# Recurrence of a selective scan: products and turn in one TensorE step with 64x64 diagonals

## The chip, the cores and the metric

The kernel runs on one core of one Trainium2 chip. The metric is the device time of one execution in microseconds (us). Engines are named as the profile names them: PE (TensorE matmul), PEld (TensorE weight load), DVE (VectorE), ACT (ScalarE), POOL (GpSimd), SP (SyncE, which here issues DMAs).

## The reference, cut to what matters

Four layers run one after another on an image of 2 x 128 x 128 pixels with 128 channels: window attention, a Fourier layer with a feed-forward, a complex-valued recurrence, and a four-direction selective scan. The change lies in the fourth. Its scan, for each of four directions k and each of 256 channels d with 16 states n, is

```
delta = softplus(delta + delta_bias)
def step(h, inp):                      # over time
    ut, dt, bt, ct = inp
    dA = jnp.exp(dt[..., None] * A4)
    h = dA * h + (dt * ut)[..., None] * bt[:, :, None, :]
    y = jnp.einsum('bkdn,bkn->bkd', h, ct)
    return (h, y)
```

So per time step and direction there are 256 x 16 states; `dA` is a factor for each of them, and the term added is the product of `delta u` (by channel) and `B` (by state). Two of the four directions go through the pixels by columns, and two of them backwards. The image is scanned in 32 x 32 windows.

## The kernel before, in words

`layer3_conv` (L1120 to L1242) makes the convolved input u, window by window, and stores it in DRAM twice with channels on partitions (`xs`, one copy by rows and one by columns) and once with pixels on partitions (`xst`, 1024 pixels x 256 channels a window).

`layer3_scan` (L1245 on) goes through 256 parts: 2 images x 4 directions x 16 windows x 2 halves of 512 time steps (T = 512). A part has eight slots, and a slot is four scans of 128 x 512: 128 partitions hold 4 states x 32 channels, so 32 such tiles make up a part's 256 x 16 states. The whole stage is written out in order by hand: `in_order` chains each engine's instructions in the order of the program text, so nothing is moved by a scheduler. Slot g issues, in this order:

- `exponentials(g + 1)` (L1518): four ACT activations of 128 x 512, dA from the spread delta `db` and a scale by partition.
- `kept(g - 1)` (L1594): ACT copies the last column of the four scanned tiles into the state kept for the next part.
- `products(g + 2)` (L1537, L1542): delta u (`du`, time on partitions) times B (`bt`, by partition), for a quarter of the states and half of the time, eight instructions of 128 x 256; of the 64 of a part ACT does 50 and POOL 14. The result `but` has time on partitions.
- `weighted(g - 1)` (L1600): POOL multiplies the four scanned tiles by C (`cb`), 128 x 2048 in one instruction.
- `tiles(g)`: four times, four PE transposes (L1574) turn 128 x 128 blocks of `but` into a PSUM tile `ups` of 128 x 512 (three buffers of one bank), and DVE scans it (L1582, `tensor_tensor_scan`: state = da * state + ups).
- `sums(g - 2)` (L1556): four PE matmuls with the selector `sel` (128 x 32) add up the states into `yps`, one for each 32 channels, on four column tiles.

A table `steps` places the rest of a part's work at slots relative to the part's first, at the head or end of a slot or after its scan number 0 to 3: `load_x` and `load_u` (SP loads), `project` (L1346) and `projected` (L1355, a DVE copy of 40 x 512 out of PSUM, and a store of C to DRAM), `turn_b` (L1364) and `turned_b` (L1371), `ranks` (L1378), `softplus` (L1389, ACT, with a change of the activation table before and after), `spread` (SP: delta to DRAM and back into `db` and `cb`, spread over partitions), `turn` (L1416) and `turned` (L1426: du = u times delta, DVE), `skip` (L1448, L1453, DVE), and for the backward directions `unturn` (L1477) and `store` (L1487, two DVE copies of 128 x 512, then a store of the pixels). PSUM's eight banks go to `ups` (3), `yps` (2) and a pool `ps_m` for the rest (3).

Of the kernel before, what the change touches and what calls it, by code (L numbers as in the profile page):

```python
# [16 lines left out]
NB = 2  # L17
# [1102 lines left out]
def layer3_conv(tc, cs, ins, x3, xs, xst, sc, sh):  # L1120
# [11 lines left out]
    with ExitStack() as ctx:  # L1132
# [20 lines left out]
        for b in range(NB):  # L1153
            for hg in range(4):
# [62 lines left out]
                for wg in range(4):  # L1217
# [24 lines left out]
                    nc.sync.dma_start(xst[b, hg, wg].rearrange("(t p) d -> p t d", p=P), xt)  # L1242


def layer3_scan(tc, cs, ins, xs, xst, yc, ys):  # L1245
# [13 lines left out]
    with ExitStack() as ctx:  # L1259
# [6 lines left out]
        five = pool("l3b_five", 5)  # L1266
        ps_u = pool("l3b_ps_u", 3, space=PSUM)
        ps_y = pool("l3b_ps_y", 1, space=PSUM)
        ps_m = pool("l3b_ps_m", 3, space=PSUM)
# [15 lines left out]

        dsk = w.tile([P, 2, 2, 2], F32, name="dsk")
# [28 lines left out]

        def load_x(i):
            b, k, s, sub = parts[i]
            _, (hg, wg) = place(i)
            xc = four.tile([P, 2, T], F32, name=f"xc_{tag_of(i)}", tag="xc")
            nc.sync.dma_start(xc, xs[k % 2, b, hg, wg, :, :, sub * T : sub * T + T])  # L1320
            held[i] = {"xc": xc}

        def load_u(i):
            b, k, s, sub = parts[i]
            _, (hg, wg) = place(i)
            ut = one.tile([P, 4, 256], F32, name=f"ut_{tag_of(i)}", tag="ut")
            px = xst[b, hg, wg]
            if k % 2:
                cols = px.rearrange("(h t w) d -> w h t d", h=32, w=4)
                for w4 in range(4):  # L1330
                    nc.sync.dma_start(
                        ut[32 * w4 : 32 * w4 + 32], cols[w4, :, 4 * sub : 4 * sub + 4, :]
                    )
            else:
                nc.sync.dma_start(
                    ut, px.rearrange("(t p) d -> p t d", p=P)[:, 4 * sub : 4 * sub + 4, :]
                )
            held[i]["ut"] = ut
# [13 lines left out]
        def projected(i):  # L1352
            v = held[i]
            xd = xds[i % 2]
            nc.vector.tensor_copy(xd[0:NX, :], v["xps"][0:NX, :])  # L1355
            v["cd"] = dr.tile([NS, T], F32, name=f"cd_{tag_of(i)}", tag="cd")
            nc.sync.dma_start(v["cd"], xd[DR + NS : NX, :])
            v["xd"] = xd

        def turn_b(i):  # L1360
            v = held[i]
            v["bps"] = ps_m.tile([P, 4, NX], F32, name=f"btps_{tag_of(i)}", tag="misc")
            for j in range(4):
                nc.tensor.transpose(  # L1364
                    v["bps"][:, j, :], v["xd"][0:NX, j * P : (j + 1) * P], cs.ident[0:NX, 0:NX]
                )
# [42 lines left out]
        def turn(g):  # L1409
            def f(i):  # L1410
                v = held[i]
                tps = ps_m.tile([P, 2, 2, P], F32, name=f"dltps_{tag_of(i)}_{g}", tag="misc")
                for j in range(2):
                    for e in range(2):
                        p0 = (2 * g + j) * P
                        nc.tensor.transpose(tps[:, j, e, :], v["dl"][:, e, p0 : p0 + P], cs.ident)  # L1416
                v.setdefault("tps", []).append(tps)
            return f
# [62 lines left out]
        def store(i):  # L1481
# [4 lines left out]
            for g in range(2):  # L1486
                nc.vector.tensor_copy(  # L1487
# [7 lines left out]
            (-12, "end", load_x), (-10, "end", load_u),  # L1495
            (-8, 1, project(0)), (-8, 2, project(1)), (-7, 0, projected),
            (-6, 0, turn_b), (-6, 1, ranks(0)), (-6, 2, ranks(1)),
            (-5, "head", softplus), (-5, 0, turned_b), (-5, 1, spread),
            (-4, 0, turn(0)), (-4, 1, turn(1)), (-3, 0, turned(0)), (-3, 1, turned(1)),
            (6, "end", load_forth), (9, 3, skip(0)), (10, 3, skip(1)),  # L1500
# [9 lines left out]

        def exponentials(g):
            i, s = divmod(g, 8)
            q, e = divmod(s, 2)
            k = parts[i][1]
            da = three.tile([P, 4, T], F32, name=f"da_{tag_of(i)}_{s}", tag="da")
            for j in range(4):
                c = 8 * q + 4 * e + j
                nc.scalar.activation(  # L1518
                    da[:, j, :], held[i]["db"][:, 4 * e + j, :], AF.Exp, scale=na[:, k, c : c + 1]
# [3 lines left out]
        def products(g):  # L1523

            i, s = divmod(g, 8)
            q, half = divmod(s, 2)
            v = held[i]
            but = five.tile([P, 2, 8, 4, 32], F32, name=f"but_{tag_of(i)}_{s}", tag="but")
            v[("but", q, half)] = but
            bt = v["bt"]  # L1530
            du = v["du"].rearrange("p t (g c) -> p t g c", c=32)
            for j in range(2):
                tb = 2 * half + j
                for n in range(4):
                    c = DR + 4 * q + n
                    if n == 3 and (tb < 3 or q % 2):
                        nc.gpsimd.tensor_tensor(  # L1537
                            but[:, j, :, n, :], du[:, tb],
                            bt[:, tb, c : c + 1].unsqueeze(2).to_broadcast([P, 8, 32]), ALU.mult,
                        )  # L1540
                    else:
                        nc.scalar.activation(  # L1542
                            but[:, j, :, n, :], du[:, tb], AF.Copy, scale=bt[:, tb, c : c + 1]
                        )

        def sums(g):
            i, s = divmod(g, 8)
            q, e = divmod(s, 2)
            v = held[i]
            if q == 0:  # L1550
# [3 lines left out]
            hs = v.pop(("hs", s))  # L1554
            for j in range(4):
                nc.tensor.matmul(  # L1556
                    v["yps"][e][32 * j : 32 * j + 32, :], sel, hs[:, j, :],
                    start=(q == 0), stop=(q == 3),
                )

        def tiles(g):
            i, s = divmod(g, 8)
            q, e = divmod(s, 2)
# [5 lines left out]
            hs = three.tile([P, 4, T], F32, name=f"hs_{tag_of(i)}_{s}", tag="hs")  # L1569
            c0 = 8 * q + 4 * e  # L1570
            for j in range(4):
                ups = ps_u.tile([P, T], F32, name=f"ups_{tag_of(i)}_{s}_{j}", tag="ups")
                for tb in range(4):
                    nc.tensor.transpose(  # L1574
                        ups[:, tb * P : (tb + 1) * P],
                        v[("but", q, tb // 2)][:, tb % 2, 4 * e + j].rearrange("p n c -> p (n c)"),
                        cs.ident,
                    )
                o, a, u = hs[:, j, :], da[:, j, :], ups
                if rev:  # L1580
                    o, a, u = o[:, ::-1], a[:, ::-1], u[:, ::-1]
                nc.vector.tensor_tensor_scan(  # L1582
                    o, a, u, state[:, c0 + j : c0 + j + 1], ALU.mult, ALU.add
                )
                at(g, j)
            v[("hs", s)] = hs

        def kept(g):

            i, s = divmod(g, 8)  # L1590
# [5 lines left out]
        def weighted(g):  # L1596
            i, s = divmod(g, 8)
            v = held[i]
            hs = v[("hs", s)]
            nc.gpsimd.tensor_tensor(  # L1600
                hs, hs, v["cb"][:, s // 2, :].unsqueeze(1).to_broadcast([P, 4, T]), ALU.mult
# [3 lines left out]
        with in_order(tc):  # L1605
            for g in range(-15, slots + 7):
# [5 lines left out]
                at(g, "mid")  # L1612
                if 0 <= g + 2 < slots:
                    products(g + 2)
# [7 lines left out]
                if 0 <= g - 2 < slots:  # L1622
                    sums(g - 2)
# [118 lines left out]
def program(tc, ins, out):  # L1742
    nc = tc.nc
    with ExitStack() as ctx:
# [7 lines left out]
        xst = dram.tile([NB, 4, 4, 1024, 256], F32, name="xst")  # L1752
# [102 lines left out]
```

## Time and profile before

| | us |
|---|---|
| median of 3 runs | 18088.65 (18087.1 to 18094.28) |
| profiled execution, its own time | 18087.3 |
| its span, first to last instruction | 18085.5 |
| first and last start of a scan (L1582) | 6150.6 and 17564.9 |

The mean granted TensorE clock of the profiled execution is 0.921. Over the whole span PE is busy 79%, DVE 84%, ACT 82% and POOL 65%; the scan stage is the last two thirds, and there the shares are higher. In a line of the profile's groups stand source line, engine, operation, output and inputs, shapes and count, then busy time and mean duration (ns) of one, then idle time before it and what ended it. In a line of the order of time stand start, duration of a run of like instructions, engine, line, and their number (x4); start-to-start times can be read off from it. A PE matmul on fp32 data that isn't a transpose appears as two records, and so does its weight load.

### The profile page before, as it was taken

To read this page: it belongs to the slowest core of one execution; us is meant where nothing else is said; L and a number is where in the kernel's file an instruction comes from. 1 tells how busy PE (TensorE), PEld (TensorE's weight loads), DVE (VectorE), ACT (ScalarE), POOL (GpSimd) and SP (SyncE) were. 2 spreads that over 40 slices of the span, in tenths; PEclk is the share of its full clock that TensorE was granted. 3 is DMA by queue.
4 is the path that set the end of the run, shared out by engine and by line. 5 is a ranking of instruction groups with operands and counts; after the bars stand their busy time and mean duration, and the time that the engine had idled before them with its cause. 6 is when DMAs were issued, how large, how long until landed. Compare 5 with 4: busy or idle time off the path is not lost. (4 is left out here: it accounts for less than half of the span.)

```text
span 18085.5 us, 277215 instructions
## 1 busy us (share of the span) xinstructions
PE 14352.7 (79%) x97794; PEld 8372.0 (46%) x97794; DVE 15201.1 (84%) x19449; ACT 14804.6 (82%) x29537; POOL 11720.3 (65%) x6490
## 2 busy tenths in 40 slices
PE   7888888888667777788877778877778887778878
PEld 5555555674223344444444444444444444444445
DVE  5766666345998899999999999999999999999986
ACT  4665666324555799999999999999999999999984
POOL 0000000011000399999999999999999999999981
PEclk9999999889889899999999999999999989999989
DMA  2000000121114544455544455554455555455556
GB/s 45 24 22 24 17 17 17 56 74 54 53 55 153 178 118 119 123 131 132 132 118 118 119 131 131 131 125 118 118 126 130 132 128 122 118 121 129 129 136 192
DMA packets 1232635, 1859.30 MB, mean 103 GB/s; under 512 B 124877, under 2 KB 591565, under 8 KB 1228942
## 3 DMA queue, kind: packets, MB, share of 16 engines
q1 hardware_dynamic: 1157374, 1817.40, 38.8%
q10 hardware_dynamic: 73872, 24.16, 0.5%
q8 instruction: 776, 12.71, 0.3%
q14 instruction: 613, 5.02, 0.1%
HBM read 1396.64 MB, written 444.60 MB: 102 GB/s over the span
## 5 line engine op out<-in xcount | busy, mean ns | idle before, releaser
L1582 DVE TENSOR_TENSOR_SCAN hs<-da,states,ups 128x512 f32<-128x512 f32 x8192 | 9845.1, 1258 | 761.8 <-PE ups L1574 746.7
L1600 POOL TENSOR_TENSOR hs<-hs,cb 128x2048 f32<-128x2048 f32 x2048 | 9327.2, 4554 | 153.9 <-ACT states L1594 151.4
L1574 PE MATMUL ups<-ident,but 128*128 128x128 f32 x32768 | 5572.7, 301 | 1913.2 <-DVE hs L1582 1334.7
L1574 PEld LDWEIGHTS ups<-ident,but 128*128 128x128 f32 x32768 | 3905.8, 151 | 5401.7 <-DVE hs L1582 3557.5
L1542 ACT ACTIVATE but<-du,bt 128x256 f32<-128x256 f32 x12800 | 5328.9, 496 | 2.4 <-DVE du L1426 1.8
L1518 ACT ACTIVATE da<-db,na 128x512 f32<-128x512 f32 x8192 | 5220.9, 709 | 3.1
L1556 PE MATMUL yps<-hs,sel 128*32 128x512 f32 x16384 | 2370.6, 653 | 509.8 <-POOL hs L1600 506.4
L1537 POOL TENSOR_TENSOR but<-du,bt 128x256 f32<-128x256 f32 x3584 | 2145.5, 619 | 10.2 <-DVE du L1426 10.2
L306 POOL TENSOR_TENSOR xres<-xres,rowb 128x256 f32<-128x256 f32 x128 | 94.3, 737 | 2466.9 <-DMA xres<-in_x 1956.5
L391 ACT COPY pT<-tps 128x512 f32<-128x512 f32 x1280 | 722.1, 584 | 1111.7 <-PE tps L386 1111.6
L386 PE MATMUL tps<-ident,s 128*128 128x128 f32 x8192 | 1229.6, 288 | 434.0 <-DVE pT L389 269.2
L358 DVE CUSTOM_DVE_ANT_1 s<-sps,relbias 128x512 f32<-128x512 f32 x2048 | 1320.5, 682 | 138.5 <-PE sps L341 133.0
L386 PEld LDWEIGHTS tps<-ident,s 128*128 128x128 f32 x8192 | 901.3, 144 | 1028.2 <-issue 499.0
L371 ACT ACTIVATE s<-s,nm 128x1024 f32<-128x1024 f32 x1024 | 1163.7, 1138 | 129.3 <-DVE nm L369 126.5
L1556 PEld LDWEIGHTS yps<-hs,sel 128*32 128x32 f32 x16384 | 332.7, 111 | 939.1 <-POOL hs L1600 711.9
L1156 POOL MEMSET xpad<- 128x34 f32 x8 | 1.3, 163 | 1169.0 <-PE xs L1030 1104.6
L341 PE MATMUL sps<-kc,qT 32*128 32x512 f32 x4096 | 619.3, 673 | 1.9 <-DVE qT L326 1.2
L389 DVE COPY pT<-tps 128x512 f32<-128x512 f32 x768 | 527.4, 687 | 59.2 <-PE tps L386 57.1
L1346 PE MATMUL xdps<-xc,xpw 128*40 128x512 f32 x1024 | 541.1, 610 | 13.2 <-DMA xpw<-in_x_projT 13.2
L734 POOL TENSOR_TENSOR xr<-xr,row_ln_b 128x512 f32<-128x512 f32 x64 | 81.2, 1270 | 708.6 <-DMA xr<-x 475.8
L1378 PE MATMUL dtps<-xd,dtw 65*128 65x512 f32 x1024 | 526.6, 595 | 0.0
L404 PE MATMUL ops<-pT,v 128*32 128x128 f32 x16384 | 500.3, 274 | 0.0
(283 smaller groups left out, 15132.6 us busy)
## 6 DMA issues: line engine op xcount, KB each, us to landing
db<-dd SPq DMA_DIRECT2D x1024, 512.0 KB
cb<-cd SPq DMA_DIRECT2D x1024, 256.0 KB
xc<-xs SPq DMA_DIRECT2D x256, 512.0 KB
dd<-dl SPq DMA_DIRECT2D x256, 512.0 KB
ut<-xst SPq DMA_DIRECT2D x128, 512.0 KB
yc<-ysb SPq DMA_DIRECT2D x128, 512.0 KB
yf<-yc SPq DMA_DIRECT2D x128, 512.0 KB
ys<-yt SPq DMA_DIRECT2D x128, 512.0 KB
```

What stands on the lines that cost most here:

```text
L341: nc.tensor.matmul(sps, v["qT"][hp, qt * P : (qt + 1) * P], kc[b, wh + g][hp, ww : ww + 2].rearrange("p a r c -> p (a r c)"), start=True, ...
L358: nc.vector.tensor_tensor_reduce(blocks(v["s", qt][:, h, 512 * g : 512 * g + 512]), blocks(v["sps", qt, g][h]), bias[:, h, :, r0 : r0 + WS ...
L371: nc.scalar.activation(s[:, h, :], s[:, h, :], AF.Exp, bias=nm[:, 2, h : h + 1], scale=-1.0, accum_out=v["sums"][:, qt, h : h + 1],)
L386: nc.tensor.transpose(tps[:, j, :], v["s", qt][:, h, k0 : k0 + P], cs.ident)
L391: nc.scalar.copy(dst, tps)
L1518: nc.scalar.activation(da[:, j, :], held[i]["db"][:, 4 * e + j, :], AF.Exp, scale=na[:, k, c : c + 1])
L1537: nc.gpsimd.tensor_tensor(but[:, j, :, n, :], du[:, tb], bt[:, tb, c : c + 1].unsqueeze(2).to_broadcast([P, 8, 32]), ALU.mult,)
L1542: nc.scalar.activation(but[:, j, :, n, :], du[:, tb], AF.Copy, scale=bt[:, tb, c : c + 1])
L1556: nc.tensor.matmul(v["yps"][e][32 * j : 32 * j + 32, :], sel, hs[:, j, :], start=(q == 0), stop=(q == 3),)
L1574: nc.tensor.transpose(ups[:, tb * P : (tb + 1) * P], v[("but", q, tb // 2)][:, tb % 2, 4 * e + j].rearrange("p n c -> p (n c)"), cs.ident,)
L1582: nc.vector.tensor_tensor_scan(o, a, u, state[:, c0 + j : c0 + j + 1], ALU.mult, ALU.add)
L1600: nc.gpsimd.tensor_tensor(hs, hs, v["cb"][:, s // 2, :].unsqueeze(1).to_broadcast([P, 4, T]), ALU.mult)
```

## The change

The product and the turn become one matmul. For each time block of 128 steps and each state, `diagonals` makes a matrix with B on its diagonal: `mask` (two 64 x 64 identities, one above the other) times B by partition, so 128 x 64 (`dg`: 4 time blocks x 8 states x 64). A matmul of 64 time steps of `du` (32 channels, as weights) with such diagonals gives 32 channels x 64 time steps of delta u B, already turned. One instruction does this for two states (128 columns), and a slot's half has 32 of them: 4 time blocks x 2 halves of 64 rows x 4 states, on 64 x 32 tiles of the array, eight tiles in all. A PSUM tile `ups` is now 128 x 1024 (two banks, one for each half of the rows), holds two scans' input interleaved, and has two buffers; a matmul's column j goes to word 8 j, and the scan reads every second word.

To go with that:

- A time block is every fourth step (`steps_of`), so partitions hold step 4 j + t. `turn_b` and `turn` read with a step of four words; `xst` gets a second copy by columns, written by four more stores a window, and a part's load of u is one DMA in which each partition has 4 KB in one piece.
- A slot is now two groups of 32 channels by two quarters of the states. The sums come two slots' worth at a time, after odd slots only (`sums(g - 2, 0)`, `sums(g - 2, 1)`); `hs` has four buffers in place of three.
- Of a part's eight `diagonals` steps six are eight ACT instructions of 128 x 64 each, and two are one POOL instruction of 128 x 512. They run five slots ahead.
- The copies of `projected` and `store` go from DVE to ACT.
- Several steps come a slot earlier, and `ps_m` has two buffers in place of three.

The number of `da`, scan, kept and weighting instructions stays. The arithmetic is the reference's.

```diff
@@ layer3_conv
-                    nc.sync.dma_start(xst[b, hg, wg].rearrange("(t p) d -> p t d", p=P), xt)
+                    nc.sync.dma_start(xst[0, b, hg, wg].rearrange("(t p) d -> p t d", p=P), xt)
+                    cols = xst[1, b, hg, wg].rearrange("(w t h) d -> h w t d", t=8, h=4)
+                    for h in range(4):
+                        nc.sync.dma_start(cols[h], xt[32 * h : 32 * h + 32])
@@ layer3_scan
-        five = pool("l3b_five", 5)
-        ps_u = pool("l3b_ps_u", 3, space=PSUM)
+        ps_u = pool("l3b_ps_u", 2, space=PSUM)
-        ps_m = pool("l3b_ps_m", 3, space=PSUM)
+        ps_m = pool("l3b_ps_m", 2, space=PSUM)
+        nc.vector.tensor_tensor(mask, cs.ident[:, 0:64], cs.ident[:, 64:128], ALU.add)
+        def steps_of(rows, tb):
+            return rows.rearrange("p (j t) -> p t j", t=4)[:, tb]
...
-            nc.vector.tensor_copy(xd[0:NX, :], v["xps"][0:NX, :])
+            nc.scalar.copy(xd[0:NX, :], v["xps"][0:NX, :])
...
-                nc.vector.tensor_copy(
+                nc.scalar.copy(
                     yt[:, 2 * g : 2 * g + 2, :], v["ytps"][g].rearrange("p j e d -> p j (e d)")
...
-            (-12, "end", load_x), (-10, "end", load_u),
-            (-8, 1, project(0)), (-8, 2, project(1)), (-7, 0, projected),
-            (-6, 0, turn_b), (-6, 1, ranks(0)), (-6, 2, ranks(1)),
-            (-5, "head", softplus), (-5, 0, turned_b), (-5, 1, spread),
+            (-13, "end", load_x), (-10, "end", load_u),
+            (-9, 1, project(0)), (-9, 2, project(1)), (-8, "head", projected),
+            (-8, 1, turn_b), (-7, 0, turned_b), (-7, 1, ranks(0)), (-7, 2, ranks(1)),
+            (-6, "head", softplus), (-6, 1, spread),
-            (6, "end", load_forth), (9, 3, skip(0)), (10, 3, skip(1)),
+            (6, "end", load_forth), (8, 3, skip(0)), (10, 3, skip(1)),
...
+        def diagonals(g):
+            i, s, qp, tb = slot_of(g)
...
+            dg = v[("dg", qp)]
+            bt = v["bt"][:, tb, DR + 8 * qp : DR + 8 * qp + 8]
+            if tb == 3:
+                nc.gpsimd.tensor_tensor(
+                    dg[:, tb], mask.unsqueeze(1).to_broadcast([P, 8, 64]),
+                    bt.unsqueeze(2).to_broadcast([P, 8, 64]), ALU.mult,
+                )
+            else:
+                for n in range(8):
+                    nc.scalar.activation(dg[:, tb, n, :], mask, AF.Copy, scale=bt[:, n : n + 1])
...
+        def products(g, half):
...
+            ups = ps_u.tile([P, 2, 64, 4, 2], F32, name=f"ups_{tag_of(i)}_{s}_{half}", tag="ups")
+            out = ups.rearrange("p r j t q -> p r t q j")
+            for tb in range(4):
+                for r in range(2):
+                    dg = v[("dg", qp)][64 * r : 64 * r + 64, tb].rearrange(
+                        "p (q n) j -> p q n j", q=2
+                    )
+                    for n in range(4):
+                        nc.tensor.matmul(
+                            out[32 * n : 32 * n + 32, r, tb],
+                            v["du"][64 * r : 64 * r + 64, tb, 32 * row : 32 * row + 32],
+                            dg[:, :, n, :], start=True, stop=True,
+                        )
+            return ups.rearrange("p r j t q -> p (r j t) q")
...
+            for half in range(2):
+                ups = products(g, half)
+                for q in range(2):
...
                 if 0 <= g + 1 < slots:
                     exponentials(g + 1)
                 if 0 <= g - 1 < slots:
                     kept(g - 1)
-                at(g, "mid")
-                if 0 <= g + 2 < slots:
-                    products(g + 2)
+                if 0 <= g + 5 < slots:
+                    diagonals(g + 5)
                 if 0 <= g - 1 < slots:
                     weighted(g - 1)
                 if 0 <= g < slots:
                     tiles(g)
...
-                if 0 <= g - 2 < slots:
-                    sums(g - 2)
+                if g % 2 and 0 <= g - 2 < slots:
+                    sums(g - 2, 0)
+                    sums(g - 2, 1)
```

## The prediction

> **What bounds the kernel now.** First I read the page's groups, for the pace of the scan stage and who is busy in it:
>
> ```profile
> L1582 DVE TENSOR_TENSOR_SCAN hs<-da,states,ups 128x512 f32<-128x512 f32 x8192 | 9845.1, 1258 | 761.8 <-PE ups L1574 746.7
> L1600 POOL TENSOR_TENSOR hs<-hs,cb 128x2048 f32<-128x2048 f32 x2048 | 9327.2, 4554 | 153.9 <-ACT states L1594 151.4
> L1574 PE MATMUL ups<-ident,but 128*128 128x128 f32 x32768 | 5572.7, 301 | 1913.2 <-DVE hs L1582 1334.7
> L1542 ACT ACTIVATE but<-du,bt 128x256 f32<-128x256 f32 x12800 | 5328.9, 496 | 2.4 <-DVE du L1426 1.8
> L1537 POOL TENSOR_TENSOR but<-du,bt 128x256 f32<-128x256 f32 x3584 | 2145.5, 619 | 10.2 <-DVE du L1426 10.2
> ```
>
> The 8192 scans start between 6150.6 and 17564.9 us (view of tile hs), so the 256 parts of eight slots take 44.59 us each, 5.57 a slot. ACT waits for nothing; POOL's waits are small; DVE waits 747 us for products. The second view, busy time by stretches (PE, PEld, DVE, ACT, POOL), says it for one millisecond:
>
> ```profile
> 12000.00:13000.00 1000.00, 778.93 (x4785) 432.97 (x4778) 925.96 (x857) 997.05 (x2118) 992.78 (x497) 0.92 0.49 120
> ```
>
> ACT 99.7%, POOL 99.3%, DVE 92.6%: ACT and POOL bound together and DVE is next. The chain of waits shows only the kernel's tail and is no help. The third view, the order of time, gives start-to-start times; durations overlap by some 0.08 us and can't be added.
>
> ```profile
> 12008.74 2.56 ACT L1518 ACTIVATE da<-db,na 128x512 f32<-128x512 f32 x4
> 12011.21 0.18 ACT L1594 COPY states<-hs 128x4 f32<-128x4 f32 x1
> 12011.30 2.90 ACT L1542 ACTIVATE but<-du,bt 128x256 f32<-128x256 f32 x7
> 12014.10 2.55 ACT L1518 ACTIVATE da<-db,na 128x512 f32<-128x512 f32 x4
> ...
> 12002.10 4.78 DVE L1582 TENSOR_TENSOR_SCAN hs<-da,states,ups 128x512 f32<-128x512 f32 x4
> 12006.81 0.71 DVE L1448 SCALAR_TENSOR_TENSOR ysb<-xc,dsk,yps 128x512 f32<-128x512 f32 x1
> ...
> 12000.44 4.57 POOL L1600 TENSOR_TENSOR hs<-hs,cb 128x2048 f32<-128x2048 f32 x1
> 12004.95 1.21 POOL L1537 TENSOR_TENSOR but<-du,bt 128x256 f32<-128x256 f32 x2
> 12006.09 4.55 POOL L1600 TENSOR_TENSOR hs<-hs,cb 128x2048 f32<-128x2048 f32 x1
> ```
>
> So: exponential 2.47/4 = 0.618, kept copy 0.09, 128x256 scaling 2.80/7 = 0.400, scan 4.71/4 = 1.178, weighting 4.51, POOL scaling 0.57. Sums per part: ACT 32 x 0.618 + 50 x 0.400 + 8 x 0.09 + softplus with two table loads 3.7 = 44.2. POOL 8 x 4.51 + 14 x 0.57 = 44.1. DVE 32 x 1.178 = 37.7, du 2 x 0.58, skip 2 x 0.63, bt 0.21, xd 0.58, yt 0.59 (two copies, every second part; the page's means less the overlap) = 41.5. They fit 44.59.
>
> **ACT and POOL after.** Per part, 50 scalings of 128x256 become 48 of 128x64. 128x512 costs 0.618 and 128x256 0.400, so 0.238 on that line for 64 columns; the 128x4 copy's 0.09 is the lower end, 0.400 the upper. I take 0.238, the same instruction form: 11.4. ACT also gets xd and yt (1.2, at 0.6 each): 19.8 + 11.4 + 0.7 + 3.7 + 1.2 = 36.8 (30 to 44.6). Two waits come with them: xd for project(1), done some 2 into slot 7 when ACT gets there, and yt for unturn, a slot old; behind both stand exponentials that DVE needs a slot later, so I count nothing (uncovered: 0.6 each). POOL: 14 scalings become two of 128x512, 1.14 each by twice the row: 38.4.
>
> **DVE after.** xd and yt leave: 40.3. The scan now reads every second PSUM word; no row has that. du reads 512 PSUM words in 0.58; at half that pace the read would take 1.16, still under the scan's 1.178, so I take none (the other end: twice the difference between a scan's 1.25 mean and 1.178, 0.15 a scan, +4.8 a part). DVE becomes the bound, unless PE is late.
>
> **PE after**, the step that decides. Sixteen 0.11 us transposes per slot go; 64 matmuls of 64x32 by 128 columns come, 32 per half. A plain fp32 matmul here is two records (16384 records at L1556 for 8192 matmuls), so a half is 64 loads and 64 matmuls. Nearest rows, from layer 0 and the sums:
>
> ```profile
> 2003.49 1.14 PE L341 MATMUL sps<-kc,qT 32*128 32x512 f32 x8
> ...
> 2007.31 1.96 PE L404 MATMUL ops<-pT,v 128*32 128x128 f32 x64
> ...
> 12005.07 1.06 PE L1556 MATMUL yps<-hs,sel 128*32 128x512 f32 x8 [0.44 <-POOL hs L1600]
> 12006.07 1.53 PE L1574 MATMUL ups<-ident,but 128*128 128x128 f32 x12
> ```
>
> L404 is the same count, length and weight width on four column tiles: 64 records in 1.96 us less the last one's 0.27, 1.69, so 0.106 per four at once. L341 shows four row tiles doing the same: eight 512-column records in 1.07 us. Both at once, eight tiles, no row shows. If they multiply, a half takes 8 x 0.106 = 0.85; if not, 1.7. If the number of instructions is the limit, the lowest speed is the densest 5 us of this trace: 181 loads and matmuls between 152.9 and 157.9 us, 27.6 ns each, 3.5 us for a half's 128. I take h = 1.0, by the tile rows, plus a little for changes between tile shapes; ends 0.85 and 3.5.
>
> What hides it: let T be the end of slot g-1's last scan, which frees a buffer pair. PE then does the second half of slot g (h), in odd slots the sums (two groups of 1.0, against one per slot before), then the first half of slot g+1 (h), seen by DVE some 0.35 later. DVE needs it at T + 4 x 1.178 = 4.71. The chain is 2h + 2.35 = 4.35: hidden. Queued in the same PE order: in slot 7 of a part project(1) (0.86, L1378's pace) gives 5.2, late by 0.5; in slot 1 ranks(1) gives 5.2 against 4.92 (bt), late by 0.3; slot 5 has two du, no wait. Slot 3 is worst: softplus and its tables stand in ACT's order ahead of the exponentials and of kept, POOL's weighting waits for kept, and the sums for POOL. From the start of slot 1: kept and diagonals 2.0, softplus 3.7, exponentials 2.5, so kept at 8.2 and the weighting done at 12.8; slots 1 and 2 last 4.92 and 5.34 (bt, skip), so that is 2.6 into slot 3; + 2.0 + 1.0 + 0.35 = 5.9, late by 1.2. In even slots nothing stands between. Sum 2.0; with 0.2 for handing over, 40.3 + 2.2 = 42.5 per part.
>
> Strided weight loads (turn, turn_b, 12 a part): L664's strided loads take 0.313 against 0.191, +1.5 us of PE a part in slots 0 and 4, under the scans there; uncovered +375 us in all.
>
> **Moved steps and DMA.** load_x, projected (with its cd store), spread (dd, four db and four cb loads) move one slot ahead on SP's queue, in the same order; nothing waits for them there, and the DMA share is 0.49. ps_m loses its third buffer; its users of one slot never need more than two. 128 more stores in the convolution, 33.5 MB; 1 KB packets and a DMA share of 0.65 there leave room under DVE (99% busy between 5900 and 6000 us). Only the last stores, 6091 to 6112, hold the scan's start: SP's queue has 16 more issues before its loads, I take +10 us (0 to 25). ut loads become one of 4 KB packets each; off the path.
>
> **Sum.** (44.59 - 42.5) x 256 = 535; 18087.3 - 535 + 10 = 17,562, say **17,560 us**. The profiled execution's 18087.3 (span 18085.5, 1.8 outside) is 1.4 below the median 18088.65, so no correction.
>
> [...] The matmuls of before write runs of eight neighbours or more; here each column lands eight words from the last. [...]
>
> **Rivals.**
> 1. *PE's burst takes the place of ACT* (slower): row tiles don't add to column tiles, or the strided output costs double; h = 1.75. The chain in odd slots is 5.85: late by 1.8 in slot 1, 1.5 in slot 3 (longer slots let POOL catch up), 0 in slot 5, 2.0 in slot 7, together 5.3: 45.6 a part, +259 + 10 = 18,356. It decides from h about 1.5 on. For: L404's whole row. Against: L341.
> 2. *The matmuls' number binds*: 3.5 us a half gives 16 x 3.5 + sums 8 + rest 5 (project and ranks 4 x 0.86, the turns) = 69 a part, +6250: 24,350. For: nothing denser for longer in the trace. Against: L404's 13 ns each over 128 instructions.
> 3. *The change doesn't relieve ACT*: 128x64 costs as much as 128x256, ACT stays at 44.6: 18,100. Against: the 128x4 copy's 0.09.
>
> **How the numbers follow.** Forecast 0.55, own range 17,180 (41.0 a part, half of the waits above gone) to 17,900 (43.9, from h 1.3); rival 1 0.25, rival 2 0.15, rival 3 0.05. Leaving out rival 2, the range runs from 17,180 to 18,700 (rival 1 with scans or table loads a little late too). Within 0.2% is about what this measurement can't tell from no change. Faster: 0.55 and the quick edge of rival 1, 0.58; same: 0.05; slower: 0.37.
>
> **What would show it.** Right: DVE 95% busy in the scan stage with ACT near 86%; products' 64 records of a half in about 1.1 us; POOL about 90%; scans still 1.25. Wrong: DVE idle released by PE ups with records of a half over 1.7 us (rival 1) or evenly spaced near 55 ns (rival 2); 128x64 pieces at 0.4 us (rival 3); scans over 1.3.

## The result, and the profile after

| | before | after |
|---|---|---|
| median of 4 runs, us | 18087.88 (18086.61 to 18094.28) | 20075.62 (20036.97 to 20100.41) |
| profiled execution's span, us | 18085.5 | 20098.6 |
| first and last start of a scan, us | 6150.6 and 17564.9 | 6325.9 and 19578.4 |
| a part, us | 44.59 | 51.77 |
| instructions | 277215 | 728715 |
| mean granted TensorE clock | 0.921 | 0.882 |

The kernel after takes 1.1096 times as long (95% interval 1.1077 to 1.1115): slower, where 17,560 us were forecast. The spans differ by 2013 us: 175 because the scans start later, 1838 (7.18 a part) because they are slower.

The groups of the page of after, those that answer to the ones shown of before (busy time and mean ns of one, then the idle time ahead of them and what ended it):

```profile
L1596 DVE TENSOR_TENSOR_SCAN hs<-da,states,ups 128x512 f32<-128x512 f32 x8192 | 9888.1, 1262 | 2831.1 <-PE ups L1574 2142.7
L1615 POOL TENSOR_TENSOR hs<-hs,cb 128x2048 f32<-128x2048 f32 x2048 | 9292.9, 4549 | 3483.6 <-ACT states L1608 1844.5
L1574 PE MATMUL ups<-dg,du 64*32 64x128 f32 x262144 | 5367.4, 299 | 3221.1 <-DVE hs L1596 1799.8
L1543 ACT ACTIVATE dg<-mask,bt 128x64 f32<-128x64 f32 x12288 | 3097.6, 335 | 0.1
L1537 POOL TENSOR_TENSOR dg<-mask,bt 128x512 f32<-128x512 f32 x512 | 535.0, 1045 | 7.4 <-DVE bt L1369 7.4
```

And the same millisecond, busy time of PE, PEld, DVE, ACT, POOL, then clock, DMA share and GB/s:

```profile
12000.00:13000.00 1000.00, 717.83 (x21034) 425.79 (x21020) 768.82 (x699) 714.32 (x1790) 722.19 (x190) 0.87 0.44 113
```

ACT and POOL are relieved, as meant: from 99.7% and 99.3% to 71% and 72%. But DVE, which should have become the bound, fell from 93% to 77%, and PE is busy for only 72%. No engine is the bound; something that is no engine is. DVE waits for PE (2143 us instead of 747), so the next view is what PE waits for. Four lines of the list of waits of after (total us, times, longest):

```profile
DVE hs L1596 <- PE ups L1574: 2142.7, 1052, 24.0
PE ups L1574 <- DVE hs L1596: 1799.8, 1425, 2.2
PE ups L1574 <- issue: 1384.2, 546, 5.8
PE yps L1554 <- issue: 94.8, 33, 5.3
```

PE stood idle 1384 + 95 us at the products and the sums for "issue": nothing that the profile shows held it, no semaphore, no engine, no data. Before has no such line of PE at its products. (The 5848 us in e1's expectation below are these 1384 with the 4464 that the list has for the weight loads.) The order of time shows one of these stalls:

```profile
12009.71 1.80 SPq L1399 DMA_DIRECT2D db<-dd  x4
...
12011.62 1.93 SPq L1404 DMA_DIRECT2D cb<-cd  x4
...
12017.30 0.42 PE L1574 MATMUL ups<-dg,du 64*32 64x128 f32 x7
...
12021.65 1.94 PE L1574 MATMUL ups<-dg,du 64*32 64x128 f32 x57 [3.93 <-issue]
...
12023.75 2.45 DVE L1596 TENSOR_TENSOR_SCAN hs<-da,states,ups 128x512 f32<-128x512 f32 x2 [5.77 <-PE ups L1574]
...
12029.05 1.69 PE L1574 MATMUL ups<-dg,du 64*32 64x128 f32 x66 [2.06 <-issue]
```

PE stops in the middle of a half, after 7 of 64 records, and goes on 3.9 us later; ahead of 12029.05 it stops once more, for 2.1 us. Both come after spread's loads. The stretches of the same microseconds (columns as above) add the DMA engines and the clock:

```profile
12008.00:12011.00 3.00, 1.12 (x69) 0.76 (x55) 3.00 (x3) 3.00 (x7) 0.72 (x1) 1.00 0.29 90
12011.00:12014.00 3.00, 2.17 (x95) 1.79 (x94) 3.00 (x4) 2.88 (x9) 3.00 (x1) 0.78 1.02 242
...
12017.00:12020.00 3.00, 0.72 (x11) 0.15 (x7) 0.98 (x1) 2.29 (x10) 3.00 (x2) 0.92 1.08 217
12020.00:12023.00 3.00, 1.35 (x53) 1.33 (x57) 0.00 (x0) 2.58 (x5) 3.00 (x1) 0.50 1.05 221
```

From 12011 to 12026 the DMA share is 1.0: all engines are full. And one more queue uses them. The pages of before and after, packets, MB and share:

```profile
q8 instruction: 776, 12.71, 0.3%
```

```profile
q8 instruction: 2574, 42.17, 0.9%
```

451,500 more instructions are 1798 more packets of 16 KB, 65 bytes each, so a packet carries about 250 instructions; counted in the trace of after, 256.0 records of PE and PEld, waits on semaphores included, lie between the ends of two packets on average (1687 packets between 8 and 18 ms). Between 12010.0 and 12018.8 the trace has none, though PE ran through 256 instructions in about 5 us; the next one lands at 12020.2, in the middle of the stall, and PE goes on 1.5 us after it. After the stall the granted clock is 0.50. That gives a theory.

### The profile page after: what moved, and what is told of

It is laid out like the page before. It is cut to its first block, busy times and chain, and to the rows that moved or that the text cites. A ratio compares the mean times of both kernels' runs of the same rounds, so it can differ in the third digit from the quotient of the medians.

```text
span 20098.6 us, 728715 instructions
## 1 busy us (share of the span) xinstructions
PE 14945.7 (74%) x327170; PEld 9072.9 (45%) x327170; DVE 14976.2 (75%) x18938; ACT 13064.4 (65%) x29537; POOL 10238.3 (51%) x3418
## 3 DMA queue, kind: packets, MB, share of 16 engines
q8 instruction: 2574, 42.17, 0.9%
## 4 chain that ended last, share of the span: by engine, by line
PE 29%; DVE 28%; issue 13%; ACT 7%; DMA 1%; SPq 1%; POOL 0%; DVEq 0%; ACTq 0%; POOLq 0%
DVE hs L1596 20%; PE ups L1574 12%; PE yps L1554 8%; ACT da L1521 4%; PE xdps L1344 2%; PE dltps L1413 2%; PE dtps L1376 1%; DVE acc L1208 1%; DVE du L1425 1%; ACT xd L1353 1%; PE ytps L1476 1%; PE cps L1199 1%; DVE ysb L1447 0%; ACT dg L1543 0%; DVE st L1707 0%
## 5 line engine op out<-in xcount | busy, mean ns | idle before, releaser
L1574 PE MATMUL ups<-dg,du 64*32 64x128 f32 x262144 | 5367.4, 299 | 3221.1 <-DVE hs L1596 1799.8
L1574 PEld LDWEIGHTS ups<-dg,du 64*32 64x32 f32 x262144 | 4234.9, 115 | 5241.9 <-issue 4463.6
L1543 ACT ACTIVATE dg<-mask,bt 128x64 f32<-128x64 f32 x12288 | 3097.6, 335 | 0.1
L1554 PE MATMUL yps<-hs,sel 128*32 128x512 f32 x16384 | 2513.2, 718 | 101.8 <-issue 94.8
L1608 ACT COPY states<-hs 128x4 f32<-128x4 f32 x2048 | 394.2, 192 | 3051.7 <-DVE hs L1596 3037.1
L1554 PEld LDWEIGHTS yps<-hs,sel 128*32 128x32 f32 x16384 | 544.8, 124 | 1593.7 <-issue 1458.5
L1376 PE MATMUL dtps<-xd,dtw 65*128 65x512 f32 x1024 | 577.6, 646 | 188.1 <-DVE bt L1369 187.5
L1344 PE MATMUL xdps<-xc,xpw 128*40 128x512 f32 x1024 | 610.0, 681 | 44.9 <-DMA xpw<-in_x_projT 25.9
L1537 POOL TENSOR_TENSOR dg<-mask,bt 128x512 f32<-128x512 f32 x512 | 535.0, 1045 | 7.4 <-DVE bt L1369 7.4
## 6 DMA issues: line engine op xcount, KB each, us to landing
cb<-cd SPq DMA_DIRECT2D x1024, 256.0 KB
```

The lines of the kernel that those rows point to most:

```text
L1344: nc.tensor.matmul(v["xps"][0:NX, :], xpw[:, k, e, :], v["xc"][:, e, :], start=(e == 0), stop=(e == 1),)
L1376: nc.tensor.matmul(ps, dtw[:, k, e * P : (e + 1) * P], v["xd"], start=True, stop=True)
L1543: nc.scalar.activation(dg[:, tb, n, :], mask, AF.Copy, scale=bt[:, n : n + 1])
L1554: nc.tensor.matmul(v["yps"][e][32 * j : 32 * j + 32, :], sel, v[("hs", s - 1 + j // 2)][:, 2 * (j % 2) + q, :], start=(qp == 0 and q == 0) ...
L1574: nc.tensor.matmul(out[32 * n : 32 * n + 32, r, tb], v["du"][64 * r : 64 * r + 64, tb, 32 * row : 32 * row + 32], dg[:, :, n, :], start=Tr ...
```

## The experiments

**Theory 1:** PE gets its instructions by DMA, 256 at a time. Its 277 records in a slot (54 before; both of PE and PEld) need a packet every 5 us while it runs (26 before); once a part spread's 3 MB keep the DMA engines full for some 15 us, the packet comes late, and PE runs dry. **Theory 2:** the order costs it: POOL's late weighting, the sums and products behind it, project and ranks with two buffers of `ps_m`. **Theory 3** (added with e3): every fetch stops PE for a time, whatever else is transferred. In the expectations the 64 of a half and e2's 32 are records of the profile; e1's 8 and e7's 16 are matmuls of the program, which the profile records twice each. So e1 has a quarter of the products' instructions and not an eighth, and e7 half of them and not a quarter. e1 to e6, e9 and e10 are one execution each; the executions of one kernel lie up to 63 us apart here.

**e1_wide8**

```diff
-            for tb in range(4):
                 for r in range(2):
...
-                            out[32 * n : 32 * n + 32, r, tb],
-                            v["du"][64 * r : 64 * r + 64, tb, 32 * row : 32 * row + 32],
-                            dg[:, :, n, :], start=True, stop=True,
+                        out[32 * n : 32 * n + 32, r],
+                        v["du"][64 * r : 64 * r + 64, 0, 32 * row : 32 * row + 32],
+                        dg[:, :, :, n, :], start=True, stop=True,
```

> The kernel after, with the 64 matmuls of a half replaced by 8 of 512 columns each: the same columns pass through the same eight tiles, with an eighth of the instructions. What it leaves out: the weights of the first block of steps stand for all four blocks, so the values of delta u times B are wrong for three of them. Theory 1 (TensorE runs out of instructions: they are fetched by DMA, 16 KB at a time, and once a part the fetch stands behind the transfers of spread): the idle time of the products put down to issue falls from 5848 us to under 600, a part from 51.77 to 43 (42 to 44.6), the whole to 17,850 us (17,600 to 18,260). Theory 2 (the order: weighting, sums and the products behind them, project and ranks with two buffers): a part stays at 50 or more and the whole at 19,600 or more, since the streaming time of a half and every wait for another engine are unchanged.

**e2_wide32** (the same with `out[..., r, tb : tb + 2]` for `tb` 0 and 2)

> The kernel after, with two blocks of steps in one matmul of 256 columns, 32 matmuls for a half instead of 64. What it leaves out: the second block of each pair is multiplied by the first one's delta u, so its values are wrong. Theory 1: TensorE takes some 160 instructions in a slot instead of some 290, so what it holds lasts nearly twice as long behind the same transfers; the two stalls of 6 us in a part nearly go: 44.5 us for a part (43 to 47), 18,240 us in all (17,850 to 18,900). Theory 2: no change, 19,600 us or more.

Measured: e1 18331.6 us, 44.87 a part; e2 18289.2 us, 44.69 a part. Waits of e2:

```profile
DVE hs L1596 <- PE ups L1574: 612.3, 575, 23.6
PE ups L1574 <- issue: 45.8, 53, 2.2
```

1384 us became 46, with the same columns through the same tiles. In e1 no such line is left. Theory 2 falls as the cause of the 7 us: the order was the same in both. e2 was foreseen within 0.2 us a part. e1 came out above its range: it gives no more than e2, so half of the instructions is already few enough, and its 17,850 was too low for another reason (the chain in odd slots, below).

**e3_stagger**

```diff
-            (-6, "head", softplus), (-6, 1, spread),
+            (-6, "head", softplus), (-6, 1, spread),
+            (-6, 1, spread_d(0)), (-5, 1, spread_d(1)), (-4, 1, spread_d(2)), (-3, 1, spread_d(3)),
+            (-5, 3, spread_c(0)), (-4, 3, spread_c(1)), (-3, 3, spread_c(2)), (-2, 3, spread_c(3)),
```

> The kernel after, with the eight loads of spread (rows of delta four times, rows of C four times) issued one by one over five slots instead of together; bytes, matmuls and order of the engines are unchanged. Theory 1: no transfer keeps all DMA engines for 10 us any more, the fetches come in time: a part 47 us (45 to 49), 18,870 us in all (18,350 to 19,400). Theory 2: unchanged, within 150 us of 20,075. A third theory, that every fetch of 16 KB stops TensorE by itself, whatever else the DMA engines carry: unchanged too.

Measured: 20065.5 us, 51.64 a part, 1379 us of issue at the products: nothing changed. The order of time of SP's queue tells why:

```profile
12037.88 0.82 SPq L1405 DMA_DIRECT2D db<-dd  x2
...
12041.50 0.45 SPq L1415 DMA_DIRECT2D cb<-cd  x1
```

Seven of the eight loads still go out within 4 us here (the eighth stands behind the store of the pixels, some 25 us later in the parts that go backwards and 7 in the others), and the DMA share from 12044 to 12052 is 1.06. SP ran ahead of the program's slots here; a place in the text paced nothing. The burst stayed, so this run can't tell theory 1 from theory 3. (e6's expectation says of it that all eight went out within 3.6 us; it was seven.)

**e4_onecopy**

```diff
-                    cols = xst[1, b, hg, wg].rearrange("(w t h) d -> h w t d", t=8, h=4)
-                    for h in range(4):
-                        nc.sync.dma_start(cols[h], xt[32 * h : 32 * h + 32])
...
+            if k % 2:
+                cols = px.rearrange("(a m w) d -> w a m d", m=4, w=32)
+                for w4 in range(4):
+                    w0 = 16 * sub + 4 * w4
+                    nc.sync.dma_start(ut[32 * w4 : 32 * w4 + 32], cols[w0 : w0 + 4])
```

> The kernel after, without the second copy of xst: the column directions read their u from the first copy, in four loads with rows of 1 KB. If the 128 added stores before the recurrence delay its start, the scans begin at 6155 us (6145 to 6180) instead of 6326, and the whole falls by 150 to 175 us where the part stays at 51.8, less where the loads of 1 KB rows lengthen the busy stretch of the DMA engines (up to 1 us in half of the parts, 128 us). If the late start has another cause (the larger diagonals' set-up, the order at the first slots), the scans begin at 6300 or later still.

Measured: 19863.9 us. First and last start of the scans, of e4:

```profile
L1599 DVE TENSOR_TENSOR_SCAN hs<-da,states,ups x8192: 1245/1255/1283, 6147.1 to 19340.9; 128x512 f32<-128x512 f32 x200
```

6147.1 instead of 6325.9: the second copy is the whole of the late start. The rest of the 212 us goes with a part of 51.54 instead of 51.77 us; after's own runs lie 63 us apart. In after's order of time:

```profile
6052.68 0.37 SPq L1242 DMA_DIRECT2D xst<-xt  x1
6053.10 5.71 SPq L1245 DMA_DIRECT2D xst<-xt  x4
...
6108.56 1.28 DVE L1208 SCALAR_TENSOR_TENSOR acc<-xz,cv,cps 128x1024 f32<-128x1024 f32 x1 [61.36 <-ACT xz L1190]
```

The four stores of a window hold SP for 5.7 to 7.5 us while the DMA engines are full (share 0.95 from 6050 to 6100). DVE stood for 61 us there, and at the end the scan stage's first load, xc, stands behind the last stores in SP's order until 6282.

**e5_tiny**

```diff
+                for m in range(24):
+                    nc.tensor.matmul(
+                        ups[0:32, 4 * m : 4 * m + 4], sel, cs.ident[:, 4 * m : 4 * m + 4],
+                        start=True, stop=True,
+                    )
```

> The kernel before, with 24 matmuls of 4 columns added ahead of each scan's four transposes; what they write is overwritten by the transposes, so nothing is left out. They bring TensorE to some 240 instructions in a slot, near the 290 of the kernel after, while every other engine, transfer and wait of the kernel before stays. Theory 1 (TensorE's instructions are fetched by DMA, and the fetch stands behind the transfers of spread): the kernel before now shows stalls of 2 to 4 us put down to issue, with a fetch in or at the end of each, once or twice in a part: 44.6 becomes 47.5 us (46 to 50.5), the whole 18,840 us (18,450 to 19,600). The other reading, that instructions cost only the time in which TensorE carries them out: 24 pairs at about 30 ns are 0.7 us for a scan, 2.9 us in a slot, beside TensorE's idle time: 44.6 to 45.2 us, 18,090 to 18,250.

Measured: 39712 us, 129 a part. Both readings missed: PE is the bound, 4.0 us a scan. 48 pairs of load and matmul on one tile, one behind the other, took up to 84 ns each (4.0 us by 48; the granted clock was 0.631 on average) and not 30. The run says nothing on the fetch.

**e6_paced** (e3 with `nc.scalar.dma_start` for the eight loads)

> The kernel after, with the eight loads of spread issued by ScalarE's queue, one in half a slot, so that ScalarE's own order holds them apart. (In e3 SyncE's queue issued all eight within 3.6 us, since nothing but their buffers holds SyncE back; so e3 had not tested what it was meant to.) Theory 1, the fetch behind a burst: no burst is longer than one load of 512 KB, about 2.4 us; the issue idle of the products falls by at least a third, a part is 47.5 us (45.5 to 49.5), the whole 18,990 us (18,450 to 19,500); ScalarE loses up to 3.5 us a part to the issuing, of which it has 14 idle. Third theory, each fetch stops TensorE whatever the DMA engines carry: 51.8 or more, 20,050 us or more.

Measured: 19027.1 us, 47.54 a part, against 18,990 and 47.5 expected. Its waits:

```profile
DVE hs L1609 <- PE ups L1587: 1144.9, 913, 4.9
PE ups L1587 <- issue: 708.3, 632, 4.4
```

Same bytes, same matmuls, 708 us instead of 1379: the burst matters. Theory 3 would have left it.

**e9_nospread**

```diff
+            if i < 2:
...
+                    nc.sync.dma_start(dbs[i][32 * n : 32 * n + 32], src)
...
+            v["db"], v["cb"] = dbs[i % 2], cbs[i % 2]
```

> The kernel after, with the eight loads of spread made for the first two parts alone; all later parts use those rows of delta and C again, so their values are wrong and 3 MB of transfers a part are left out. TensorE's instructions, 290 in a slot, are unchanged. Theory 1 (the fetch of instructions stands behind these transfers): the stalls go although every instruction is still fetched: 44.7 us for a part as in e2 (44 to 45.5), 18,280 us in all (18,090 to 18,500). Third theory (each fetch of 16 KB stops TensorE by itself for a time): a good part of the stalls stays, 46.5 us or more, 18,750 us or more.

Measured: 18241.7 us, 44.51 a part, in the middle of theory 1's range:

```profile
DVE hs L1597 <- PE ups L1575: 532.5, 531, 23.4
PE ups L1575 <- issue: 117.4, 173, 3.4
```

All instructions are fetched (2574 packets, as in after), and over 90% of the stalls are gone. So neither the number of instructions nor the transfers cost the time alone: e2 takes half of the one away, e9 the other, and either frees 7.1 to 7.3 us a part. Theory 3 falls.

**e10_tiny4**

```diff
+                for m in range(16):
+                    n, c0 = m % 4, 4 * (m // 4)
+                    nc.tensor.matmul(
+                        ups[32 * n : 32 * n + 32, c0 : c0 + 4], sel, cs.ident[:, c0 : c0 + 4],
+                        start=True, stop=True,
+                    )
```

> e5 again with a cheaper addition: the kernel before with 16 matmuls of 4 columns ahead of each scan's transposes, spread over four tiles of the array instead of 24 on one tile (in e5 the pair of load and matmul took some 65 ns on the one tile and TensorE became the bound by itself, so e5 said nothing of the fetch). What they write is overwritten, nothing is left out. Each is recorded twice, 64 instructions for a scan, some 300 in a slot. Theory 1: stalls put down to issue of 2 to 4 us, once or twice in a part, as in the kernel after: 48 us for a part (46 to 51), 18,950 us (18,450 to 19,750). If instructions cost only their own time, and the four tiles work side by side: 32 pairs at 16 ns are 0.5 us for a scan, hidden: 44.6 to 45.5 us, 18,090 to 18,320. If the four tiles do not overlap, 2.1 us for a scan: TensorE is the bound again at over 80 us a part, and the run says nothing.

(Against what is said there, the addition changes the values that come out; why, no run shows.) Measured: 20287.1 us, 53.18 a part, over the range of theory 1. In its waits the stalls appear, in a kernel that had none:

```profile
PE ups L1575 <- issue: 899.1, 391, 5.5
PE ups L1580 <- issue: 114.5, 54, 4.8
```

1014 us are 4.0 a part, of 8.6 more. The rest I put down to PE's own work, 89% busy from 12000 to 13000 us; that isn't tested. So many instructions bring the stalls into the kernel before too, and my estimate of the added work was too low a second time; as a measure of the fetch alone the run is only half good.

**e7_d128 and e8_tuned**

```diff
-                            v["du"][64 * r : 64 * r + 64, tb, 32 * row : 32 * row + 32],
+                        v["du"][:, tb, 32 * row : 32 * row + 32],
...
-            (-9, 1, project(0)), (-9, 2, project(1)), (-8, "head", projected),
-            (-8, 1, turn_b), (-7, 0, turned_b), (-7, 1, ranks(0)), (-7, 2, ranks(1)),
+            (-14, 1, project(0)), (-14, 2, project(1)), (-13, "head", projected),
+            (-8, 0, turn_b), (-8, 3, turned_b), (-7, 1, ranks(0)), (-7, 2, ranks(1)),
...
-            (13, 2, unturn(0)), (13, 3, unturn(1)),
+            (14, 0, unturn(0)), (14, 1, unturn(1)),
```

The first two lines are e7's, the others what e8 adds.

> A whole kernel with a quarter of the instructions: 128x128 diagonals of B in four tiles of the array (128 rows by 32 columns), matmuls of 256 columns, 16 for a half; the steps lie in two banks of 256 so that one matmul stays in one bank; u from a single copy; diagonals four slots ahead in two buffers. All of the computation is there. Theory 1: the stalls go as in e1 and e2, ScalarE's copies rise from 0.24 to about 0.29 us (48 in a part: +2.4 us) and GpSimd's from 1.05 to about 2.1 us, neither becomes the bound: a part 44 us (43 to 45.5), scans from 6155, 17,920 us in all (17,660 to 18,300). Theory 2 has fallen. If ScalarE or GpSimd does become the bound, 45.5 us or more and 18,300 or more.

> e7 with four steps moved out of the slots in which e2 still showed waits: project to slot 2, projected to slot 3, the transposes of B and their copy to slot 0, unturn to slot 6. All of the computation is there. Expected from e2's slots: 2.0 us of slot 5 in the later half of the parts, 1.0 to 1.6 us of slot 7 and 0.75 us of slot 1 go: 42.4 us for a part (41.5 to 43.8), 17,510 us in all (17,280 to 17,870), which would be 3% below the kernel before. If the waits only move to other slots, no change against e7.

Measured: e7 18791 us (1.039 times before, 1.0372 to 1.0407), 47.28 a part; e8 18241 us (1.0085, 1.007 to 1.010), 45.19; both are above their ranges. The stalls went, as said (27 us of issue in e7), but e7's stretch shows what came instead:

```profile
12000.00:13000.00 1000.00, 915.05 (x12784) 468.33 (x12780) 876.06 (x793) 843.63 (x1998) 860.46 (x215) 1.00 0.48 117
```

PE is 91.5% busy. My step was wrong: four tiles of 128 rows with 256 columns are twice the work of eight of 64 rows with 128, since a 128x128 diagonal has twice the zeros for each value; a half takes 1.9 us (1.15 in after). The moved steps gave 2.1 us a part, of some 3.0 that e2's slots had promised.

**e11_evened and e12_bybuf**

```diff
+                db = one.tile([P, 2, T], F32, name=f"db_{tag_of(i)}_{h}", tag=f"db{h}")
...
+                cb = one.tile([P, 2, T], F32, name=f"cb_{tag_of(i)}_{h}", tag=f"cb{h}")
...
+            (-5, 0, spread_d(0)), (-4, 0, spread_d(1)), (-3, 0, spread_d(2)), (-2, 0, spread_d(3)),
+            (-3, 1, spread_c(0)), (1, 0, spread_c(1)),
```

That is e12's; e11 has one `db` and one `cb` with two buffers, as after, and twelve loads on ScalarE's queue.

> The kernel after with what e4, e6 and e8 point to, all of the computation in place: u from a single copy (e4), spread's loads in pieces of 256 KB from ScalarE's queue, two or three in a slot (e6, finer), and the moved steps of e8. Theory 1: from e6's 47.5 us the 2.0 us of slot 5 in the later half of the parts (1.0 on average), 1.3 of slot 7 and 0.75 of slot 1 go, and about half of the stalls that e6 kept (1.5 of some 3): 43.5 us for a part (42.5 to 45.2), 17,790 us in all (17,540 to 18,250). If pieces of 256 KB still fill the DMA engines when they meet the loads and stores of SyncE's queue, the stalls of e6 stay: 44.5 to 45.5 us, 18,050 to 18,300.

> The kernel after with all of its computation, the moved steps of e8 and the single copy of u of e4, and spread's loads held apart without ScalarE's queue (in e11 its twelve issues a part, 0.3 to 0.45 us each, made ScalarE late): the rows of delta lie in four tiles and those of C in two, each with one buffer, so that SyncE can issue the loads of a tile only when the slots that used it are over, 512 KB in a slot over six slots. Theory 1: TensorE's idle time put down to issue at the products, 1384 us after, 708 in e6 and 510 in e11, falls to 300 or less, and with e9's waits less the 1.0 us of slot 5, 1.0 of slot 7 and 0.75 of slot 1 a part takes 43.2 us (42.3 to 45), 17,720 us in all (17,490 to 18,180), below the kernel before. If SyncE, which now waits for ScalarE and GpSimd, delivers u, x or the rows of delta late, waits on DMA appear at the exponentials or at the weighting and a part takes 45 us or more, 18,180 or more.

Measured: e11 18299 us (1.0117, 1.010 to 1.0134), 45.42 a part, 510 us of issue: over theory 1's range by 49 us and inside the other reading's, though the stalls fell from e6's 708. ScalarE now stands for 20% of the chain of waits (7% after). Ahead of its exponentials the trace shows a wait that e6 doesn't have:

```profile
ACT da L1541 <- DMA ut<-xst: 628.2, 154, 7.1
```

It falls where ScalarE issues loads while the loads of u run, so its twelve issues can be behind it, as e12's expectation has it; no run shows that they are. e12 17876.5 us, 0.9888 of before (0.9871 to 0.9904), 43.72 a part. Its waits:

```profile
DVE hs L1618 <- PE ups L1596: 707.9, 566, 5.3
PE ups L1596 <- issue: 355.3, 384, 4.2
```

With all matmuls of after in place, buffers that SP has to wait for hold the loads apart without another engine's queue; together with the single copy and the moved steps that makes the kernel 1.1% faster than before. The stalls are not quite gone: 355 us, where 300 or less were expected.

## Why the prediction was wrong

Mean duration of each slot, us (from its first scan to the next slot's, so a wait ahead of a slot counts with the slot before), the forecast as the prediction's scans, DVE work and waits give it, without the 0.2 for handing over:

| slot | 0 | 1 | 2 | 3 | 4 | 5 | 6 | 7 | part |
|---|---|---|---|---|---|---|---|---|---|
| forecast | 5.34 | 5.2 | 5.34 | 5.9 | 4.71 | 5.87 | 4.71 | 5.2 | 42.3 |
| after | 5.32 | 5.76 | 5.32 | 8.78 | 7.77 | 7.92 | 4.86 | 6.06 | 51.8 |
| e9, no spread | 5.32 | 5.76 | 5.35 | 5.49 | 4.73 | 6.82 | 4.82 | 6.23 | 44.5 |
| e12 | 5.62 | 5.13 | 5.33 | 5.44 | 4.72 | 5.91 | 4.88 | 6.71 | 43.7 |

- **The failed step** is in "Moved steps and DMA": spread's transfers go on SP's queue, "nothing waits for them there, and the DMA share is 0.49". PE waited for them. The share is a mean of full and empty stretches (0.29 and 1.08 stand among those of after above), and I asked only who needs the data, not who else needs the engines. After less e9 is 7.3 us a part, all of it in slots 3 to 5; spread's loads run from the end of slot 2 into slot 4.
- **The number of instructions** I weighed only as time in which PE carries them out (the densest row, 27.6 ns). That was rival 2, and it came out neither by its mechanism nor by its price: PE took 64 records of a half in 1.15 us including the last one's 0.27, 13.8 ns each. What counted in these runs is how long 256 of them last. Spread keeps the DMA engines full for 15 us or more in before (12013 to 12029 us, a share of 1.03 to 1.08) and in after (12011 to 12026) alike, and e2 has the same eight loads; 256 records last about 26 us in before, 9.5 in e2 and 5 in after, and only after stalls for long. When a fetch is asked for, and so how long one takes from there, no run shows. The page of before had the row (q8, 776 packets), and I passed over it.
- **h = 1.0 was right**: row tiles and column tiles multiply here. Two blocks that PE wasn't kept from, of after:

```profile
12001.79 1.15 PE L1574 MATMUL ups<-dg,du 64*32 64x128 f32 x64
...
12006.59 2.03 PE L1574 MATMUL ups<-dg,du 64*32 64x128 f32 x128
```

  So 0.88 for a half, 1.15 less the last record's 0.27, where the prediction has 0.85 if they multiply and 1.7 if not. That strided output costs double, the other condition of rival 1, no run shows: these are columns that land eight words apart, at 13.8 ns from record to record. Rival 1 falls.
- **ACT, POOL, DVE after were right**: a 128x64 scaling takes 0.24 us (eight in 2.02), the POOL instruction 1.05 against 1.14, and the scan of every second PSUM word 1.256 median against 1.254. Rival 3 falls.
- **The chain in odd slots** was mis-sized: 2.2 us of waits forecast, 4.2 in e9. Slot 1 waits 0.84 instead of 0.3, slot 7 1.5 instead of 0.5 (project and the sums are both there, e12's move of project leaves another wait), and slot 5 0.93 where none was forecast: in the half of the parts that go backwards unturn needs the two buffers of `ps_m` that hold delta until du has been made (in e9 6.0 us in the other half, 7.7 in these; in e8, with unturn moved, 5.9 in all). So "ps_m's users never need more than two" was wrong too. Slot 3 was 0.8, with 1.2 forecast. So even without the stalls the change as it stands gains next to nothing: e9 with a single copy would be 18,241.7 - 179 = 18,063 us, by sum.
- **The start**, "+10 us (0 to 25)", was 175, all of it the second copy (e4). DVE's 99% between 5900 and 6000 us, from which I took that there was room, is not what the last windows look like: DVE is idle from 6050 to 6100 us in after, at a DMA share of 0.95, while SP issues the stores.

In sum: 175 + 7.18 x 256 = 2013 us, of which 1479 are PE's idle time for issue at products and sums (117 of it also in e9). The rest of the 7.3 us a part, some 2 us, I put down to the clock after a stall and to what stands behind it: behind the one shown above it was 0.50, and 57 records took 1.94 us where 64 took 1.15 at a clock of 1.00; in the 2 us after the 336 stalls of over 1.2 us between 8 and 18 ms it was 0.53 in the median. That is read off the trace and not tested by a run of its own.

## What to carry to other kernels

A packet of q8 came for each 256.0 records of PE and PEld in after and for each 255.9 in before. Before multiplying PE's instructions, divide 256 by its records per microsecond and look for long stretches at a DMA share of 1.0. Behind stretches of some 15 us PE stalled where 256 records lasted 5 to 6 us (after, e10) and hardly where they lasted 9 to 10 (e2, e7); in between nothing was run. Where they last as short as in after, make the instructions fewer or hold the transfers apart: of after's 1384 us of issue at the products the first left 46 (e2), the second 708 (e6) and 355 (e12). Transfers were held apart by something the queue must wait for, single buffers (e12) or another engine's order (e6), not by their place in the program (e3, 1379 us). Idle time that the profile puts down to "issue", in the middle of a block of independent work, is where to look for this.

## What the runs showed of the hardware

- Packets of 16 KB on q8 go with PE's records: in after, 256.0 records of PE and PEld, waits on semaphores included, lie between the ends of two of them on average (8 to 18 ms), and in before 255.9 (8 to 17 ms). Of 336 stalls of over 1.2 us put down to issue at after's products between 8 and 18 ms, the number of such records between the end of the last fetch and the stall is exactly 256 in 160, less in 12 and 510 at most; where a fetch lands in the stall (324), PE goes on 1.2 to 1.6 us after it (5th to 95th of 100).
- Eight tiles of 64 rows by 32 columns work side by side: 64 fp32 records of 128 columns in 0.88 us at a granted clock of 1.00 (after, from 12001.79 us).
- Loads and matmuls of four columns on one tile took up to 84 ns a pair at a granted clock of 0.631 (e5), where 64 pairs of 128 columns on eight tiles took 13.8 ns each at a clock of 1.00 (after).
- Issuing a store of 32 partitions took SP 1.47 us (median of 128) over after's windows of the convolution, where the DMA share lay between 0.39 and 0.95; one of 128 partitions took 0.37 there (median of 32, up to 1.16).
